# The first strip's output projection of layer one, moved from an even unit into the odd unit behind it, with its sum kept on chip for layer two

## The chip, the cores and the metric

The kernel runs on one core of a Trainium2 chip. Five engines work side by side, each on its own stream of instructions: TensorE (PE in the profile; its weight loads are PEld), VectorE (DVE), ScalarE (ACT), GpSimd (POOL) and SyncE (SP), which here only issues DMAs. The metric is the device time of one execution in microseconds; of several runs the median is given.

## The reference, cut to what matters

The input x has 8 images of 384 channels and 64 x 64 points, in float32. Two layers follow each other, each with a residual and a group normalisation (groups of 12 channels over all points of an image) in front:

- Layer one: `x = x + L0(gn(x))`. L0 normalises every point over its channels, makes q, k and v with one matrix, and does attention in 8 x 8 windows with 8 heads. Half of the heads use plain windows; the other half use windows shifted by 4 rows and 4 columns, with wrap-around and a mask. The two halves are joined and go through a 384 x 384 output projection, `out @ proj_w + proj_b`.
- Layer two: `x = x + L1(gn(x))`. L1 is a 1 x 1 convolution, a filter in the frequency domain of 8 x 8 patches, a 3 x 3 convolution per channel, a gate `gelu(x1) * x2`, and a 1 x 1 convolution back.

What matters here: the group normalisation of layer two needs the mean and the variance of a whole image of layer one's result. Layer two of an image can begin only when the last of its points has gone through layer one's output projection, residual included.

## The kernel before, in words

An image is cut into 8 strips of 8 rows. A strip is a tile of 128 partitions x 3 x 512 floats (768 KB). A strip of layer one has two branches, the plain windows (br 0) and the shifted ones (br 1). One branch of one strip is a *unit*; 16 units make an image, and unit 2s + br of an image belongs to strip s and branch br. Below, units of image b are counted from `first = 16 b`, and the units 16, 17 and 18 of an image are the units 0, 1 and 2 of the next one: there layer one of the next image runs while layer one of this image is completed. Layer two of image b runs two units and more behind its layer one, beside layer one of image b + 1.

The order of the work is a written plan. `at(place, piece, *args)` puts a piece (a small function) at a place, a number in units. All pieces are sorted by place and called in that order. Matmuls stay in exactly that order, since `matmul` marks each with `keep_in_program_order`; the instructions of the other engines are ordered by a scheduler of the framework, which follows the plan and its own estimates. [...]

The pieces of a unit of layer one: `qk_tile` (pq, three tiles of three matmuls, which ACT moves out with their bias), `v_tile` (pvv), `scores` (pS), `weights` and `exponent` (the softmax, on DVE and ACT, tile e), `turn` (transpose, pT), `apply` (pA), `normalise` (DVE: rc and o) and `put` (transpose, po, copied into oT). Ahead of it, once in a strip, `group_normal` reads a loaded strip x_norm and makes y (line 328), `ln_square` makes sq (ACT and POOL), `ln_sums`, `ln_scale` and `shifted_half` finish the normalised strip. The pieces of layer two: `normal_x1` (ACT: xn from x_mix, line 574), `mix` (pt), `transform` (pf), `back` (pz, moved by ACT into z), `conv` (DVE: zz, line 673, eight instructions per third of a strip), `gate` (g) and `finish` (pw, added by DVE onto x_finish, line 712, and stored).

The pieces around the change:

- `load(b, s, what)` takes a new tile out of the pool with tag x (5 buffers) and issues a DMA of 768 KB on SyncE's queue (line 309). The kinds are stats, norm and add (from the input x) and mix and finish (from x1d, the result of layer one, kept in DRAM). Most transfers wait for one ACT instruction of each unit, the second move of the unit's first pq (`zs["gate"]`), so that they start in dense matmul work.
- `project(b, s, m)` does a third of the output projection: three matmuls into pr, and one DVE instruction that adds bias and residual in x_add (line 546).
- `keep(b, s)` takes the statistics of the strip with three DVE instructions (st, line 237); `store(b, s)` writes the strip to x1d (line 556).
- `second_mean(b)` closes the statistics: DVE makes mv_b (line 244), TensorE multiplies it with a group matrix (pm_b, one small matmul), DVE makes gt_b. `second_std(b)` multiplies again (pv_b), ACT takes the root (sd_b), DVE makes gs_b and sh.

Why strip 0 is late: the shifted windows of the last strip wrap around into strip 0, so oT of strip 0 is complete only in unit 16. The strips 0 and 7 of an image are both projected there:

```python
places = [first + 2 * NS + f + (0.0 if s else 0.24) for f in (0.36, 0.44, 0.52)]
```

The pools set further conditions. PSUM has four banks for all tiles made by `psum` (pq, pvv, pr, pt, pf, pz, pm_b, pv_b and the first two thirds of pw), used in turn, and two double banks made by `psum2` (pS, pT, pA, po and the last third of pw), also in turn. A tile's first matmul waits until the tile that had its bank before has been read.

TensorE's stream also holds no-ops (`nc.tensor.nop`). The planner at the end of the function counts TensorE's instructions and spreads empty ones over the tiles of pq and pr, so that the runs of many small matmuls (ln, pf, pz, pA, pS) begin at a chosen place within blocks of 256 instructions.

Of the kernel before, what the change touches and what calls it, by code (L numbers as in the profile page):

```python
# [18 lines left out]
NS = SW // WS  # L19
# [19 lines left out]
def block_kernel(ctx: ExitStack, tc: tile.TileContext, out, x, consts, fsel, wqk, wv, bqk, bv,  # L39
                 wp, bp, lng, lnb, rpb1, rpb2, w_in, w_dw, w_out, filt):  # L40
    nc = tc.nc
    B = x.shape[0]
# [32 lines left out]
    def strip(tag, bufs, name):  # L75
        return sb.tile([P, KC, ST], F32, tag=tag, bufs=bufs, name=name)
# [7 lines left out]
    def rows_of(img, s):  # L84

        return img[:, s * WS:(s + 1) * WS, :].rearrange("(p k) h w -> p k (h w)", k=KC)
# [190 lines left out]
    def at(place, piece, *args):  # L277
        plan.append((place, len(plan), piece, args))

    xs, ys, y2s, qks, vs, os_, ots, x1s, zs = ({} for _ in range(9))  # L280
# [12 lines left out]
    def in_dense_work(i):  # L293


        if zs.get("gate"):
            behind(i, zs["gate"], mybir.DependencyClass.Sync, "transfer in dense work")
# [4 lines left out]
    def load(b, s, what):  # L302

        if b == 0 and (what == "stats" or what == "norm" and s < 3):
            xs[b, s, what] = first_x[s]
            return
        t = xs[b, s, what] = strip("x", 5, f"x_{what}_{b}_{s}")
        src = x1d[b][s] if what in ("mix", "finish") else rows_of(x[b], s)
        in_dense_work(nc.sync.dma_start(out=t, in_=src))
# [411 lines left out]
    for b in range(B):  # L721
        first = 2 * NS * b

        for s in range(NS):
            u = first - 14.84 + s if b else -10 + 0.1 * s
            at(u, load, b, s, "stats")
            at(u + (0.5 if b else 0.05), input_stats, b, s)
        if b == 0:
            at(-3.02, pack_qk)
            at(-2.9, qk_weights, 0)  # L730
            at(-0.95, v_weights)
            at(-0.94, qk_weights, 1)
            at(-0.9, position_bias, 0)
            at(-0.5, position_bias, 1)
            at(0.2, out_bias)
            at(0.2, filter_weights)
        at(first - 5.8 if b else -8, input_mean, b)
        at(first - 5.4 if b else -7.9, input_std, b)
        for s in range(NS):
            u = first + 2 * s  # L740

            v = u - 4
            at(v - 0.84, load, b, s, "norm")
            at(v + 0.15, group_normal, b, s)
            at(v + 0.45, ln_square, b, s)
            if b:
                at(v + 0.985, small_tiles, v + 1)
            at(v + 0.99, ln_sums, b, s)
            at(v + 1.35, ln_scale, b, s)

            if s:
                at(v + 1.50, shifted_half, b, s - 1, 1)
            else:
                at(u - 1.15, shifted_half, b, NS - 1, 1)
            at(u - 1.2 if s < NS - 1 else v + 1.55, shifted_half, b, s, 0)
            for br in range(2):
                w = u + br
                for t in range(3):
                    at(w - 1 + (0.14, 0.34, 0.55)[t], qk_tile, b, s, br, t)
                for g in range(2):  # L760
                    at(w - 1 + ((0.78, 0.86), (0.67, 0.88))[br][g], v_tile, b, s, br, g)
                at(w + 0.05, scores, b, s, br)
                at(w + 0.12, weights, b, s, br)
                at(w + 0.30, exponent, b, s, br)
                at(w + 0.64, turn, b, s, br)
                at(w + 1.00, apply, b, s, br)
                at(w + 1.07, normalise, b, s, br)
                at(w + 1.23, put, b, s, br)

            if 0 < s < NS - 1:  # L770
                places = [u + 3 + f for f in (0.27, 0.45, 0.70)]
            else:
                places = [first + 2 * NS + f + (0.0 if s else 0.24) for f in (0.36, 0.44, 0.52)]
            at(int(places[0]) - 0.84, load, b, s, "add")
            for m in range(KC):
                at(places[m], project, b, s, m)
            at(places[2] + 0.1, keep, b, s)
            at(int(places[2]) + 1.15, store, b, s)
        first += 2 * NS
        at(first + 1.25, second_mean, b)  # L780
        at(first + 1.90, second_std, b)
        if b == B - 1:
            at(first + 2, tap_matrices)
        for s in range(NS):
            u = first + 2 + 2 * s
            at(u - 0.84, load, b, s, "mix")
            at(u + 0.02, normal_x1, b, s)
            for i in range(4):
                at(u + (0.28, 0.45, 0.60, 0.78)[i], mix, b, s, i)
            for j in range(2):  # L790
                at(u + (0.995, 1.02)[j], transform, b, s, j)
            if b < B - 1:
                at(u + 1.985, small_tiles, u + 2)
            at(u + 1.99, back, b, s)

            for n, m in enumerate((0, 2, 1)):
                for tap in range(1, 6):
                    at(u + (2.62, 3.15, 3.5)[n] + 0.06 * tap, conv, b, s, m, tap)
                for tap in range(6, 9):
                    at(u + 4.2 + 0.25 * (n * 3 + tap - 6) / 9, conv, b, s, m, tap)  # L800
            if b == B - 1:
                at(u + 2.3, conv_taps, b, s)
            at(u + 5.16, load, b, s, "finish")
            at(u + 4.5, gate, b, s)
            at(u + 6.10, finish, b, s)
# [130 lines left out]
```

## Time and profile before

| what | value |
|---|---|
| median of 3 runs | 3713.88 us (3712.17 to 3715.45) |
| the profiled execution, whole | 3717.37 us |
| its span in the profile | 3715.4 us |
| granted TensorE clock | 0.995 |
| DMA | 377.34 MB, mean 102 GB/s |
| DVE: one zz (line 673) | 751 ns, 1490 of them |
| DVE: one x_add with pr (line 546) | 747 ns, 192 of them |
| DVE: one st of x_add (line 237) | 689 ns median |
| DVE: mv_b (line 244) | 805 ns |
| DVE: one y (line 328) at the boundary | 541 ns median |
| store of x1d, loads of x_mix | 64 each, 768 KB each |

The profile is one execution, taken by the hardware. Busy times are per engine; a line number is that of the kernel shown here. Because of the helper `matmul`, all matmuls have line 62 and all transposes line 72, so groups are told apart by their tiles: `pr<-oT,wp_sb` is pr written from oT and wp_sb. A float32 matmul stands as two records, so a tile of three matmuls is x6. The ends of matmuls are modelled, so TensorE's time is best read from the start of one tile to the start of the next. Consecutive instructions on DVE overlap a little at their ends too, and their cost is the step from start to start. A wait is put down to whoever released it last. The chain of waits goes back from an end to what released each step, and "issue" in it is time in which nothing visible was waited for.

### The profile page before, as it was taken

What the parts mean: (1) busy time and instruction counts of PE and PEld (TensorE: products, weight loads), DVE (VectorE), ACT (ScalarE), POOL (GpSimd) and SP (SyncE); (2) the same over time, 40 slices, a digit from 0 to 9 for tenths busy, and PEclk for the clock granted to TensorE, in tenths of its full rate; (3) what the DMA queues carried; (4) which work ended last, traced back from release to release, by engine and by line L of the source; (5) the groups of instructions that cost most, each with busy time, mean ns of one, the idle gap of its engine ahead of it and who ended that gap; (6) DMA issues with size and microseconds to landing.
All of it is one profiled execution on the core that took longest, in us unless ns stands there. A gap on an engine that the chain in (4) does not pass through costs nothing.

```text
span 3715.4 us, 92922 instructions
## 1 busy us (share of the span) xinstructions
PE 3609.1 (97%) x38528; PEld 2340.4 (63%) x38528; DVE 2844.0 (77%) x4601; ACT 2383.0 (64%) x3946; POOL 435.1 (12%) x776
## 2 busy tenths in 40 slices
PE   4999999999999999999999999999999999999898
PEld 2666666666666666666666666666666666666554
DVE  4555568777887788787887778877788777777898
ACT  1766676666676576675776667676676766676442
POOL 5111111011111011101111011111011111110000
PEclk9999999999999999999999999999999999999999
DMA  4222222233232233222332332323232322222422
GB/s 122 80 89 75 92 100 102 87 111 109 101 123 84 89 134 109 104 94 104 107 130 84 109 106 101 132 82 105 88 131 102 107 89 84 100 81 81 154 103 77
DMA packets 144507, 377.34 MB, mean 102 GB/s; under 512 B 12308, under 2 KB 12900, under 8 KB 144100
## 3 DMA queue, kind: packets, MB, share of 16 engines
q1 hardware_dynamic: 139952, 370.60, 28.4%
q8 instruction: 319, 5.23, 0.6%
q0 software_dynamic: 2048, 0.15, 0.1%
q10 hardware_dynamic: 2100, 0.63, 0.1%
q14 instruction: 88, 0.72, 0.1%
HBM read 270.54 MB, written 100.79 MB: 100 GB/s over the span
## 4 chain that ended last, share of the span: by engine, by line
PE 86%; DVE 6%; DMA 4%; ACT 2%; issue 1%; POOL 0%; SPq 0%; DVEq 0%; ACTq 0%; POOLq 0%
PE pq L62 24%; PE pr L62 13%; PE pvv L62 12%; PE pt L62 12%; PE pw L62 6%; DVE zz L673 3%; PE pS L62 3%; PE pA L62 3%; PE pT L72 3%; PE po L72 3%; PE pz L62 3%; PE pf L62 2%; PE ln L62 2%; DMA x_norm<-in_x_dram 1%; DMA rpb_raw<-in_rpb_dram 1%
## 5 line engine op out<-in xcount | busy, mean ns | idle before, releaser
L673 DVE SCALAR_TENSOR_TENSOR zz<-z,dw_sb,zz 128x512 f32<-128x512 f32 x1490 | 1081.8, 751 | 23.7 <-ACT z L632 11.2
L62 PE MATMUL pq<-y,wqk_sb 128*128 128x512 f32 x2160 | 990.2, 596 | 0.0
L62 PEld LDWEIGHTS pq<-y,wqk_sb 128*128 128x128 f32 x2160 | 402.7, 190 | 437.1 <-issue 403.9
L62 PE MATMUL pt<-wi_sb,xn 128*128 128x384 f32 x1536 | 534.6, 486 | 0.0
L62 PE MATMUL pr<-oT,wp_sb 128*128 128x512 f32 x1152 | 523.1, 592 | 0.4 <-DVE oT L537 0.4
L62 PE MATMUL pvv<-wv_sb,y 128*128 128x192 f32 x2880 | 495.8, 326 | 0.0
L62 PEld LDWEIGHTS pvv<-wv_sb,y 128*128 128x128 f32 x2880 | 471.7, 190 | 36.2 <-issue 22.0
L394 ACT ACTIVATE qab<-pq,bq_sb,cst 96x512 f32<-96x512 f32 (+1 forms) x256 | 197.8, 772 | 401.9 <-PE pq L62 385.0
L62 PEld LDWEIGHTS pt<-wi_sb,xn 128*128 128x128 f32 x1536 | 286.1, 190 | 200.9 <-issue 44.0
L394 ACT ACTIVATE kcd<-pq,vec 32x512 f32<-32x512 f32 x512 | 348.4, 680 | 9.0
L62 PEld LDWEIGHTS pr<-oT,wp_sb 128*128 128x128 f32 x1152 | 211.1, 190 | 223.8 <-issue 212.3
L376 POOL COPY y<-y 128x384 f32<-128x384 f32 x112 | 100.0, 893 | 1529.4 <-PE pvv L62 1035.9
L335 POOL TENSOR_TENSOR sq<-sq 128x512 f32<-128x512 f32 x128 | 164.3, 1283 | 638.2 <-ACT sq L333 633.3
L584 ACT COPY t<-pt 128x384 f32<-128x384 f32 x256 | 124.1, 485 | 177.7 <-PE pt L62 174.5
L667 ACT ACTIVATE zz<-z,dw_sb 128x512 f32<-128x512 f32 x183 | 134.0, 733 | 159.0 <-PE pw L62 144.5
L349 DVE TENSOR_TENSOR lr<-m 128x128 f32<-128x128 f32 x64 | 19.7, 308 | 278.3 <-ACT m L347 278.3
L394 ACT ACTIVATE qcd<-pq,bq_sb,cst 96x512 f32<-96x512 f32 (+1 forms) x256 | 197.1, 770 | 44.4 <-PE pq L62 40.9
L428 ACT COPY v<-pvv 128x384 f32<-128x384 f32 x256 | 120.7, 477 | 160.2 <-PE pvv L62 159.2
L546 DVE SCALAR_TENSOR_TENSOR x_add<-pr,vec,x_add 128x512 f32<-128x512 f32 x192 | 143.4, 747 | 94.3 <-PE pr L62 92.6
L62 PE MATMUL pw<-zz,wo_sb 128*128 128x512 f32 (+1 forms) x512 | 182.4, 499 | 0.0
L394 ACT ACTIVATE kab<-pq,vec 96x512 f32<-96x512 f32 (+1 forms) x256 | 174.2, 680 | 9.0 <-PE pq L62 7.4
L72 PEld LDWEIGHTS pT<-cst,e 128*128 128x128 f32 x1024 | 119.1, 141 | 67.2 <-issue 39.8
(140 smaller groups left out, 5297.2 us busy)
## 6 DMA issues: line engine op xcount, KB each, us to landing
x_add<-in_x_dram SPq DMA_DIRECT2D x64, 768.0 KB
x1d<-x_add SPq DMA_DIRECT2D x64, 768.0 KB
x_mix<-x1d SPq DMA_DIRECT2D x64, 768.0 KB
x_finish<-x1d SPq DMA_DIRECT2D x64, 768.0 KB
out_dram<-x_finish SPq DMA_DIRECT2D x64, 768.0 KB
x_norm<-in_x_dram SPq DMA_DIRECT2D x61, 768.0 KB
x_stats<-in_x_dram SPq DMA_DIRECT2D x56, 768.0 KB
rs<-line SPq DMA_DIRECT2D x62, 256.0 KB
```

Source lines behind the costliest of these rows:

```text
L62: tc.keep_in_program_order(nc.tensor.matmul(*args, **kw))
L72: tc.keep_in_program_order(nc.tensor.transpose(*args, **kw))
L335: nc.gpsimd.tensor_tensor(sq[:, 0, :], sq[:, 0, :], sq[:, k, :], ALU.add)
L349: nc.vector.tensor_tensor(rc, m[:, 0:P], m[:, 0:P], ALU.mult)
L376: nc.gpsimd.tensor_copy(dst[:, :, :, :, 0:4], src[:, :, :, :, 4:8])
L394: return nc.scalar.activation(dst[to:to + n], pq[of:of + n], AF.Identity, bias=bias[of:of + n], scale=scale)
L428: nc.scalar.copy(v[:, 2 * g:2 * g + 2, :, 0:HD], pvv[:, 0:384].rearrange("p (g h d) -> p g h d", g=2, h=4))
L546: nc.vector.scalar_tensor_tensor(t[:, m, :], pr, bp_sb[:, m:m + 1], t[:, m, :], ALU.add, ALU.add)
L584: nc.scalar.copy(t1, pt[:, 0:C])
L667: nc.scalar.activation(zz.rearrange("p (r c) -> p r c", c=SW), z[:, 1:9, 1:SW + 1], AF.Copy, scale=dw_sb[:, m, 4:5])
L673: i = nc.vector.scalar_tensor_tensor(acc.rearrange("p (r c) -> p r c", c=SW), z[:, dy:dy + 8, dx:dx + SW], dw_sb[:, m, TAPS[tap]:TAPS[tap] ...
```

## The change

For all images but the last, the projection of strip 0 moves from unit 16 to unit 17: its three parts from the places 16.60, 16.68 and 16.76 to 17.20, 17.32 and 17.45. What hangs on these places moves along: the load of x_add for strip 0 from 15.16 to 16.16, its statistics (`keep`) from 16.86 to 17.55, its store from 17.15 to 18.15. `second_mean` moves from 17.25 to 17.57, behind the new `keep`; `second_std` stays at 17.90. The load of x_mix for strip 0 is left out: `normal_x1` reads the tile x_add of strip 0, which is still on chip, and the store to x1d stays, since `finish` reads it much later. The last image keeps the old places.

```diff
         if b == 0 and (what == "stats" or what == "norm" and s < 3):
             xs[b, s, what] = first_x[s]
+            return
+        if what == "mix" and s == 0 and b < B - 1:
+            xs[b, s, what] = xs[b, s, "add"]
             return
         t = xs[b, s, what] = strip("x", 5, f"x_{what}_{b}_{s}")
         src = x1d[b][s] if what in ("mix", "finish") else rows_of(x[b], s)
...
             if 0 < s < NS - 1:
                 places = [u + 3 + f for f in (0.27, 0.45, 0.70)]
+            elif s == 0 and b < B - 1:
+                places = [first + 2 * NS + 1 + f for f in (0.2, 0.32, 0.45)]
             else:
                 places = [first + 2 * NS + f + (0.0 if s else 0.24) for f in (0.36, 0.44, 0.52)]
             at(int(places[0]) - 0.84, load, b, s, "add")
...
             at(int(places[2]) + 1.15, store, b, s)
         first += 2 * NS
-        at(first + 1.25, second_mean, b)
+        at(first + (1.25 if b == B - 1 else 1.57), second_mean, b)
         at(first + 1.90, second_std, b)
```

In the built program the scheduler also moves work of other pieces at these boundaries. On DVE, y of the next image's strip 3 goes from behind the odd unit's zz to a place between x_add's second and third part, and the statistics of x_stats move from unit 18 into unit 17. On ACT, sq of that strip moves ahead of the evictions of the third pq, and the table load for the exponent follows DVE's e.

## The prediction

> **What bounds the kernel now.** I read the page's busy times first, then TensorE's waits, then the stages at an image boundary, then the chain of waits there. The page:
>
> ```profile
> PE 3609.1 (97%) x38528; PEld 2340.4 (63%) x38528; DVE 2844.0 (77%) x4601; ACT 2383.0 (64%) x3946; POOL 435.1 (12%) x776
> ```
>
> TensorE is busy for 97% of 3715.4 us, and the change adds and removes no matmul. It can only gain or lose through TensorE's idle time. Who ended that idle time (waits of PE over the whole run: total us, times, longest):
>
> ```profile
> PE pT L72 <- ACT e L469: 9.9, 8, 1.5
> PE pz L62 <- ACT v L428: 6.9, 13, 1.0
> PE pw L62 <- DVE o L504: 6.1, 6, 1.3
> PE pS L62 <- issue: 2.7, 5, 0.9
> ```
>
> The rest of that list belongs to the start and to the last image. These four stand at the image boundaries. I take the boundary behind the fourth image as the pattern (the others repeat it) and split it into the even unit that holds the projection now, the odd unit that gets it, and the two units behind. Windows: us, then busy time of PE, PEld, DVE, ACT, POOL, clock, DMA share, GB/s:
>
> ```profile
> 1703.80:1748.80 45.00, 45.00 (x348) 26.34 (x342) 30.08 (x50) 21.30 (x42) 3.48 (x10) 1.00 0.09 36
> 1748.80:1767.70 18.90, 18.00 (x290) 13.37 (x283) 17.06 (x28) 14.13 (x21) 2.62 (x4) 1.00 0.73 259
> 1767.70:1798.60 30.90, 29.90 (x318) 19.52 (x314) 25.59 (x46) 25.07 (x42) 3.88 (x7) 1.00 0.16 57
> 1798.60:1818.00 19.40, 17.82 (x288) 12.69 (x284) 18.63 (x27) 13.27 (x19) 2.47 (x3) 1.00 0.50 177
> ```
>
> The even unit has no idle TensorE and DVE and ACT with 15 and 24 us to spare; the odd unit is short on TensorE, nearly full on DVE (17.06 of 18.90) and full of DMA (0.73). TensorE idles 0.90, 1.00 and 1.58 us in the last three. The first two in TensorE's timeline:
>
> ```profile
> 1764.97 2.02 PE L62 MATMUL pz<-cst,t 64*64 64x64 f32 x93 [0.90 <-ACT v L428]
> ...
> 1770.77 0.66 PE L62 MATMUL pw<-g,wo_sb 64*64 64x256 f32 x8 [1.00 <-DVE o L504]
> ```
>
> The 0.90: ACT starts the odd unit's exponent only at 1757.51, then works through seven evictions of pq and one of pT, and frees pvv's bank too late. The 1.00 has a longer story, which the chain of waits through this stage tells (start, us, what):
>
> ```profile
> 1753.50 0.78 ACT qab L394
> ...
> 1754.29 3.28 DMA x1d<-x_add
> ...
> 1757.59 0.32 SPq L309
> ...
> 1757.95 9.96 DMA x_norm<-in_x_dram
> ...
> 1768.01 1.46 DVE y L328 x3
> ...
> 1769.67 0.97 DVE o L504
> ...
> 1770.77 3.44 PE pw L62 x16
> ```
>
> The store of strip 0 must land before SyncE issues x_mix of strip 0; x_norm is issued behind it and is the fifth of six transfers of 768 KB; DVE stands in y until x_norm is there; o waits behind y; pw waits for o.
>
> [...] o stands behind y on DVE though its pA was done at 1767.90, and no matmul passed the waiting pw. So a pm_b that waits holds all of TensorE. [...] the zz at 1757.40 takes 0.99 us instead of the row's 751 ns, while POOL copies y from 1756.41 to 1757.84. [...]
>
> **The change part by part.** T is the start of the odd unit's first pq, 1749.83. All sums are for one boundary; seven boundaries have the change, six of them with both layers running.
>
> *Matmuls of pr.* Three tiles of three matmuls, each tile 2.57 us (pr 1683.23, next tile 1685.81), go from the even to the odd unit: minus 7.7 and plus 7.7, sum 0. In the built program the total of PE no-ops is the same (3902); the planner spreads the odd unit's 30 over six tiles instead of three. One more PE wait instruction per image shifts where the small matmuls fall in the instruction stream by up to six; the even unit's run goes from place 180 to 145 of 256, where the like runs of the other strips stand (140 to 147). [...] I take 0, bounds minus 2 and plus 3 us for the run.
>
> *The even unit without pr.* DVE loses three x_add, three st and mv_b, all in idle stretches there (3.7 and 3.9 us idle before them). Its last tiles of pt and pvv keep their distances to their evictions, so no new wait: 0.
>
> *The load of x_mix for strip 0.* Its data were never late: xn ran 1768.00 to 1770.89 and its first pt started at 1777.50, so 6.6 us cover it. Removing it is worth nothing by itself. Its place in SyncE's queue is worth something: the store of strip 0 moves a unit back, x_mix goes, and x_norm is third behind one store and x_finish. Where three loads go in that order in later odd units, the third has landed between T+13.0 and T+14.1 (in the trace's completion marks; here x_norm came at T+18.1). The built order has DVE's y and ACT's sq of that strip one unit earlier too, before the boundary.
>
> *pz, 0.90.* With 7.7 us more TensorE work in the odd unit, ACT evicts pq as it comes (second pq ends T+11.4, third T+16.6). By my count its first pvv eviction ends at T+22.3, while pz needs it at T+23.9. Gone. Over six boundaries the gaps are 0.70, 0.71, 0.90, 0.97, 0.87, 0.98: minus 5.1 us.
>
> *pw, 1.00.* y is now done long before o. From pA's end DVE needs rc 0.25 and o 0.96 plus about 0.25 of hand-over, 1.5 us; TensorE has 1.85 us of pS and pw in between. Other even units with that distance show 0.1. The gaps 1.26, 1.20, 1.00, 0.90, 1.07, 0.71 sum to 6.1; minus 5.5 us.
>
> *pm_b, the new wait.* It stood behind the even unit with mv_b done at 1744.04, 9.3 us early. Now it follows the third pq, with mv_b behind the last x_add. TensorE reaches it at T + 2.68 + 5 x 2.57 + 0.87 = T+16.4. DVE: e ends at T+7.65 as before (same rows ahead of it). Then in the built order x_add, zz, st, zz, zz, x_add, zz, st, zz, y x3, x_add, oT, st, zz, mv_b. Steps from start to start, read from the same mix at 1689 to 1697: 0.66 after x_add or zz, 0.60 after st, 0.79 between dependent zz, 0.45 for y[...]. That brings y to T+13.8 (just after x_norm has landed), the last x_add to T+15.2, its pr being ready at T+14.0, mv_b to T+17.8; with 0.81 us it ends at T+18.6. TensorE waits 2.2 us. Bounds: 1.0 with every step at its shortest[...], 3.5 if x_norm lands at T+14.1[...]. Queued behind pm_b are pT, pvv and pz; they move by the same 2.2, and DVE and ACT catch up meanwhile, so nobody behind waits anew: sd comes at T+25.9, xn some 6 us before its pt. Six boundaries: plus 13.2 us. The first boundary has no layer two beside it (no zz); its mv_b ends near T+17.4: plus 1.0.
>
> *Store a unit later.* It delays x_stats in the unit behind by about 2 us; DVE has 3.7 us idle at 1793.09 to cover it: 0. The pT wait of the fourth unit (1.3) follows from rs, y and e of that unit, which stay as they are: 0.
>
> Sum: 13.2 + 1.0 - 5.1 - 5.5 = **plus 3.6 us**. The profiled span of 3715.4 becomes 3719.0. The profiled execution took 3717.37 us around its span; the median of the runs is 3713.88, 3.5 lower. I add the same 3.6 to the median: 3717.5 us, 0.1%. A measurement of this kernel tells about 0.2% (7.4 us) from no change.
>
> **The rivals.** *A, the trade (0.65):* two waits out, one in, as above; within 0.2% while the pm_b wait is between 0.4 and 2.8 us. *B, x_norm becomes the stall (0.28), slower:* y stands in DVE's queue ahead of the last x_add, so every us that x_norm lands behind T+13.8 adds a us to pm_b, at six boundaries. For it: the margin is half a us at best, and ACT's sq stands ahead of the qcd evictions too. Against: two of the four transfers ahead of it are gone. From T+14.4 on it is over 0.2%; at today's T+18.1 it would be 3.6 + 6 x 4.3, plus 29 us, 3743. Landing at T+15.3 gives 3726. *C, the gain is kept (0.07), faster:* DVE gets mv_b done before TensorE comes, minus 10.6 us, 3703. For it: x_add, st and mv_b alone, each dependent on the one before (0.79 + 0.79 + 0.81), would end 2.4 us after pr at T+14.0, just when TensorE comes. Against: that needs a free DVE at T+14.0, and it has y, oT and a zz to do in between. *D, the change does not reach the waits* (in B's share): pz and pw keep theirs since ACT's burst stays; then plus 14, 3728.
>
> Range: 3708 to 3727; it holds A with its bounds (1.0 and 3.5 of wait give minus 3.6 and plus 11.4) and the nearer half of B. Faster 0.07, same 0.65, slower 0.28.
>
> **What would show it.** Right: PE waits list pm_b <- DVE mv_b with some 14 us in 6 or 7 times, 2 to 2.5 each; the rows pz <- ACT v and pw <- DVE o lose some 5 us each; pT stays near 9.9; even unit near 37.3 us, odd near 28. DVE shows y without an idle before it in the odd unit. Wrong: y waiting for x_norm (B), pm_b without a wait (C), or new "issue" gaps in the small matmuls (the stream's places).

## The result, and the profile after

The changed kernel takes 3722.73 us (median of 12 runs, 3718.51 to 3728.0). The kernel before, run beside it, takes 3712.52 us (12 runs, 3707.72 to 3715.45). The ratio is 1.0028, with a 95% interval of 1.0020 to 1.0036: 10.2 us slower, between 7 and 13. Repeated later (e5) it was 3723.94 against 3713.37, 1.0029 (1.0018 to 1.0040). The prediction was 3717.5 us in a range of 3708 to 3727. The measured time lies in the range, and the trade that was forecast (two waits out, one in) came, but its size was not right: plus 3.6 us was forecast, and the change costs 0.28%, more than the 0.2% that can be told from no change.

The profiled execution took 3723.41 us around a span of 3721.6. Its difference to the profiled span before (3715.4) is only 6.2 us. That is no contradiction: the profiled execution before, 3717.37 us, lay 4.9 us above the median of its own kernel, the one after 0.7. So I compare the terms in the traces, and take sizes from the medians.

TensorE's busy time differs by 0.7 us from before (3609.1), with the same 38528 matmul records:

```profile
PE 3609.8 (97%) x38528; PEld 2342.4 (63%) x38528; DVE 2844.6 (76%) x4601; ACT 2386.4 (64%) x3946; POOL 436.2 (12%) x776
```

Who ended TensorE's idle time, kernel after (total us, times, longest):

```profile
PE pm_b L62 <- DVE mv_b L244: 16.9, 7, 2.6
...
PE pT L72 <- ACT e L472: 9.3, 8, 1.5
...
PE pS L62 <- issue: 3.9, 7, 0.9
...
PE pz L62 <- ACT v L431: 1.8, 7, 0.3
```

The row pw <- DVE o (6.1 us) is gone, pz lost 5.1 us of its 6.9, and pm_b (the matmul that closes the statistics) stands there new with 16.9. The four units at the boundary behind the fourth image, which the prediction used as its pattern (us, then busy time of PE, PEld, DVE, ACT, POOL, clock, DMA share, GB/s):

```profile
1707.50:1744.80 37.30, 37.30 (x331) 22.95 (x326) 24.98 (x43) 20.28 (x38) 1.78 (x8) 1.00 0.18 64
1744.80:1773.10 28.30, 25.66 (x310) 16.57 (x306) 25.28 (x41) 15.85 (x22) 5.48 (x6) 1.00 0.37 122
1773.10:1802.60 29.50, 29.50 (x312) 19.46 (x307) 22.74 (x39) 23.76 (x41) 1.33 (x5) 1.00 0.24 82
1802.60:1822.10 19.50, 17.91 (x292) 12.77 (x286) 18.70 (x27) 13.27 (x19) 2.47 (x3) 1.00 0.50 177
```

The even unit lost its 7.7 us, the odd one grew from 18.90 to 28.30 and now holds the idle time, and the unit behind it shrank from 30.9 to 29.5. DVE is busy 25.28 of 28.30 us in the odd unit. Here is what it does there before pm_b, with T = 1745.80, the start of the first pq (start, us, what), and then the wait on TensorE:

```profile
1759.33 1.46 DVE L331 TENSOR_SCALAR y<-x_norm,gs_a 128x512 f32<-128x512 f32 x3
1760.71 0.74 DVE L549 SCALAR_TENSOR_TENSOR x_add<-pr,vec,x_add 128x512 f32<-128x512 f32 x1
1761.48 0.69 DVE L531 COPY oT<-po 64x512 f32<-64x512 f32 x1
1762.21 0.69 DVE L237 BATCH_NORM_STATS2 st<-x_add 128x6 f32<-128x512 f32 x1
1762.82 1.44 DVE L676 SCALAR_TENSOR_TENSOR zz<-z,dw_sb,zz 128x512 f32<-128x512 f32 x1
1764.18 0.79 DVE L244 BATCH_NORM_AGGREGATE mv_b<-st 128x2 f32<-128x144 f32 x1
```

```profile
1765.03 0.38 PE L62 MATMUL pm_b<-mv_b,cst 128*128 128x1 f32 x2 [2.64 <-DVE mv_b L244]
```

y starts without an idle before it, the last x_add at T+14.9, mv_b ends at T+19.2, and TensorE had nothing to do from T+16.6 on. The sequence is the one forecast; one zz in it takes 1.44 us.

One thing has no counterpart in the waits. The odd unit lasts 28.2 to 28.3 us in four of the six images that have both layers, but 30.00 and 29.91 us in the third and the fifth (the second and fourth of these six), with no more idle time. Windows of 3.4 us through the third image's odd unit show it in the clock column:

```profile
1313.60:1317.00 3.40, 3.05 (x8) 1.02 (x6) 3.34 (x6) 3.06 (x5) 0.29 (x1) 1.00 0.28 110
1317.00:1320.40 3.40, 1.11 (x10) 1.11 (x11) 3.37 (x6) 1.97 (x3) 2.56 (x2) 1.00 0.00 0
1320.40:1323.80 3.40, 3.40 (x13) 3.40 (x12) 3.37 (x8) 1.01 (x1) 0.00 (x0) 0.50 0.02 5
1323.80:1327.20 3.40, 3.40 (x81) 3.38 (x81) 0.77 (x2) 1.44 (x3) 0.00 (x0) 0.99 0.00 0
```

TensorE is idle for 2.3 of the 3.4 us in the second window (the pm_b wait), and for the whole third window the granted clock is 0.50. TensorE is "busy" there and does half the work: the pvv matmuls behind the wait (24 records) take 5.74 us where they take 4.07 us at the fourth image:

```profile
1320.44 5.74 PE L62 MATMUL pvv<-wv_sb,y 128*128 128x192 f32 x24
...
1766.18 4.07 PE L62 MATMUL pvv<-wv_sb,y 128*128 128x192 f32 x24
```

That is 1.7 us more, with no entry in any list of waits.

### The profile page after: what moved, and what is told of

It reads as the page before. It is cut to its first block, busy times and chain, and to the rows that moved or that the text cites. A ratio compares the mean times of both kernels' runs of the same rounds, so it can differ in the third digit from the quotient of the medians.

```text
span 3721.6 us, 92896 instructions
## 1 busy us (share of the span) xinstructions
PE 3609.8 (97%) x38528; PEld 2342.4 (63%) x38528; DVE 2844.6 (76%) x4601; ACT 2386.4 (64%) x3946; POOL 436.2 (12%) x776
## 4 chain that ended last, share of the span: by engine, by line
PE 86%; DVE 8%; DMA 2%; ACT 2%; issue 2%; POOL 0%; SPq 0%; ACTq 0%; DVEq 0%; POOLq 0%
PE pq L62 25%; PE pvv L62 13%; PE pt L62 12%; PE pr L62 12%; PE pw L62 6%; DVE zz L676 4%; PE pS L62 3%; PE pA L62 3%; PE pz L62 3%; PE pT L72 3%; PE po L72 3%; PE pf L62 2%; PE ln L62 2%; DMA rpb_raw<-in_rpb_dram 1%; DMA rs<-line 1%
```

## The experiments

Each row has the kernel before as it ran beside it on the same chip.

| run | median us (runs) | before | ratio (95%) | pm_b wait, sum, us | half clock, windows of 3.41 us, images 2 to 7 |
|---|---|---|---|---|---|
| after | 3722.73 (12) | 3712.52 | 1.0028 (1.0020 to 1.0036) | 16.9 | 2 |
| e5 after again | 3723.94 (7) | 3713.37 | 1.0029 (1.0018 to 1.0040) | 16.9 | 1 |
| e1 wait filled | 3721.45 (21) | 3713.76 | 1.0020 (1.0013 to 1.0026) | 1.6 | 0 |
| e9 a third filled | 3724.75 (7) | 3713.75 | 1.0030 (1.0019 to 1.0042) | 11.7 | 2 |
| e10 wait lengthened | 3749.61 (4) | 3713.75 | 1.0097 (1.0084 to 1.0111) | 32.6 | 10 |
| e4 mean first on DVE | 3711.31 (21) | 3713.76 | 0.9992 (0.9986 to 0.9999) | 7.4 | 0 |
| e8 a load put back | 3713.75 (13) | 3713.37 | 1.0002 (0.9994 to 1.0010) | 8.8 | 0 |
| e2 pm_b later | 3709.14 (21) | 3713.76 | 0.9987 (0.9980 to 0.9993) | 0.2 | 0 |
| e6 e2 with places | 3704.46 (11) | 3713.37 | 0.9976 (0.9967 to 0.9985) | 0 | 0 |
| e7 after with places | 3722.93 (9) | 3713.37 | 1.0027 (1.0017 to 1.0036) | 17.0 | 4 |
| e3 sum kept, no move | 3714.74 (13) | 3713.76 | 0.9999 (0.9991 to 1.0007) | none | 0 |
| e11 e3, o first on DVE | 3706.44 (19) | 3712.86 | 0.9984 (0.9977 to 0.9991) | none | 0 |

The last two columns are from the one profiled execution of each. The halved windows are those between the first 110 us and 3480 us; before and after have others outside that stretch (clock 0.50 from 65 to 78 us in both).

### The clock: e1, e9, e10, e5

Theory: a wait of 2.6 us costs more than 2.6 us, since the clock may be halved behind it, as at 1320.4 us above. Three edits vary the idle time at pm_b and leave its place in the order as it is.

e1 fills the wait with matmuls of constants:

```diff
         pm = psum(f"pm_{name}")
+        for _ in range(fill):
+            matmul(pm, ident, cst[:, 0:ST], start=True, stop=True)
         matmul(pm[:, 0:1], grp, mv[:, 0:1], start=True, stop=True)
...
-        gs1[b] = group_mean(st1s.pop(b), f"b{b}")
+        gs1[b] = group_mean(st1s.pop(b), f"b{b}", 3 if 0 < b < B - 1 else 0)
```

> The kernel after, with three matmuls of constants (128x512 each, overwritten by the mean that follows) in front of pm_b in images two to six, where TensorE waits 2.48 to 2.64 us for mv_b. They take 2.57 us, as long as the wait. Theory 1, the clock: what the prediction missed is the granted clock, halved for 3.41 us after some of the waits, each time worth 1.7 us, in between none and six boundaries of one execution. Then no stretch of half clock is left between the first 100 us and 3480 us, the time falls by 1.7 us for each one taken away, to 3717 to 3720 us (the fastest execution of the kernel after was 3718.5), and its executions agree as closely as those of before (within 8 us, not 9.5). Theory 2, the clock is no matter and the rest is scattered over issue gaps: unchanged, 3722 to 3723 us.

Measured: 3721.45 us, no half clock in the middle of the run, and odd units of 28.2 to 28.8 us in all six images. (The expectations of e1, e9 and e10 name images two to six; the edits cover two to seven, six boundaries.) The trace agrees with the theory; the median does so only weakly. It is 7.7 us above before, where the kernel after was 10.2 and 10.6 above: 2.5 to 2.9 us gained, although the filled units are some 0.3 us longer than unhalved ones of after. But the intervals of the ratios overlap, it missed its 3720, and its runs still spread over 7.4 us.

e9 fills only a third:

```diff
-        gs1[b] = group_mean(st1s.pop(b), f"b{b}", 3 if 0 < b < B - 1 else 0)
+        gs1[b] = group_mean(st1s.pop(b), f"b{b}", 1 if 0 < b < B - 1 else 0)
```

> The kernel after, with one matmul of constants (0.87 us) in front of pm_b in images two to six instead of three: TensorE then idles 1.6 to 1.8 us at pm_b and not 2.6, the end of the unit stays where it is. In the profiled executions so far a free-running window of 3.41 us was followed by half clock when it held 1.79 to 2.38 us of idle, and was not at 1.66 to 1.77 (once 1.79 was, once 1.85 was not). Theory 1: an idle stretch of 1.8 us or less can't reach that in any window, so no half clock is left and the time is that of the kernel with three, 3719 to 3722 us, lost idle or not. Rival: each idle us counts toward the clock, and it lies halfway to the kernel after.

This one missed. The waits fell to 1.63 to 1.82 us, and still two windows of half clock came, behind windows that held 1.70 and 1.69 us of idle; the odd units of those two images took 29.92 and 29.90 us, the others 28.2 to 28.6. The time, 3724.75 us, is no better than after. The third image's window and the one behind it:

```profile
1315.20:1318.60 3.40, 1.70 (x12) 1.30 (x12) 3.37 (x5) 1.86 (x3) 2.37 (x2) 1.00 0.00 0
1318.60:1322.00 3.40, 3.40 (x13) 3.40 (x12) 3.33 (x9) 1.01 (x1) 0.00 (x0) 0.50 0.02 5
```

So the limit is lower than I had set it. I laid the grid of 3.413 us that the clock records give over the profiles of after, e5, e7 and e9: in images two to seven, windows with 1.69, 1.70, 1.79, 2.01, 2.19, 2.19, 2.28 and 2.38 us of recorded idle were followed by half clock, while windows with 1.66 to 1.77, and one with 1.85, were not. The least idle time followed by half clock is 1.69 us, about half of the window, but the idle time that the profile records for a window does not settle it alone up to about 2 us; e10 has an exception at 1.99.

e10 makes mv_b later:

```diff
         strip_stats(st1s[b], s, xs[b, s, "add"])
+        for _ in range(3 if s == 0 and 0 < b < B - 1 else 0):
+            nc.vector.bn_stats(st1s[b][:, KC - 1, :], xs[b, s, "add"][:, KC - 1, :])
```

> The kernel after, with the last st of strip 0 written three more times in images two to six (the same values), so that mv_b comes some 3 us later (the order then also sets three st of x_stats ahead of it): a pm_b wait of about 5.5 us instead of 2.6. Theory 1 (wait plus clock): at each of those five boundaries one or two windows of half clock, 5 to 9 in all instead of 2; 3722.7 + 5 x 2.9 + 4 to 12 = 3741 to 3749 us, and a narrower spread than after. Rival (the wait alone): 3737 us, and the number of halved windows doesn't grow.

The scheduler also set three st of x_stats ahead of mv_b, as the expectation names. This dose separates the theories. Windows through the second image's odd unit:

```profile
873.80:877.20 3.40, 0.00 (x0) 0.00 (x0) 3.40 (x7) 0.86 (x2) 1.25 (x1) 1.00 0.00 0
877.20:880.60 3.40, 2.73 (x12) 2.73 (x13) 3.32 (x8) 0.24 (x1) 0.00 (x0) 0.51 0.02 5
880.60:884.00 3.40, 3.40 (x12) 3.40 (x12) 0.36 (x2) 0.77 (x1) 0.00 (x0) 0.50 0.00 0
884.00:887.40 3.40, 3.40 (x89) 3.38 (x89) 0.00 (x0) 1.73 (x3) 0.00 (x0) 0.99 0.00 0
```

The time grew by 26.9 us to 3749.61, the pm_b wait by only 15.7 (16.9 to 32.6). The wait alone would have given 3738. The six odd units together grew from 172.9 to 200.4 us, by 27.4; what the waits leave is 11.7 us, for 8 more windows of half clock (10 instead of 2), 1.5 us each. That is a little less than 1.7: four of the ten windows also hold 0.53 to 1.62 us of the idle time itself. At the fourth image a window with 1.99 us of idle was not followed by half clock; that came only behind the next one, which was idle throughout:

```profile
1771.53:1774.94 3.41, 1.42 (x4) 0.35 (x2) 3.35 (x6) 3.24 (x4) 1.88 (x2) 1.00 0.00 0
1774.94:1778.35 3.41, 0.00 (x0) 0.00 (x0) 3.41 (x7) 0.36 (x1) 0.65 (x1) 1.00 0.00 0
1778.35:1781.76 3.41, 3.34 (x14) 3.34 (x15) 3.08 (x9) 0.85 (x1) 0.00 (x0) 0.50 0.02 5
```

Behind a window that was halved already a second one came with less idle time: with those 0.53 to 1.62 us at four of the six boundaries, and in e7 with 0.30 us at one.

e5 is the kernel after once more.

> The kernel after, unchanged, beside the kernel before on one chip with more executions. Theory 1 (the clock is halved after a random number of the pm_b waits): its profile shows some stretches of half clock between 100 and 3480 us, not the two at the same places, and the median is 3721 to 3725 us, 8 to 10 above before. If the two stretches come at the same boundaries again, their number is a property of the program and not of the execution.

Its profile had one such window, behind the fourth image, where the first profile had none. Whether a wait is hit is thus a property of the execution, and the runs of after spread over 9.5 us.

### DVE's order: e4 and e8

The prediction said why the wait is there: DVE has y, oT and a zz to do between the last pr (T+14.0) and mv_b. e4 sets y (the first i) and that zz (the second) behind mv_b:

```diff
+            if b and s == 3:
+                behind(i, zs["aggr"], mybir.DependencyClass.NoSync, "mean first")
...
+        if b < B - 2 and s == 6 and m == 1 and tap == 1:
+            behind(i, zs["aggr"], mybir.DependencyClass.NoSync, "mean first")
```

> The kernel after, with DVE's order in the odd unit changed: the three y of strip 3 and the zz of the second channel block stand behind mv_b instead of ahead of it. Theory 1: the sum's own chain (x_add, st, mv_b behind the last pr at T+14.0, with oT and one st of x_stats between) ends near T+17.4, TensorE comes at T+16.6, so the pm_b wait falls from 2.6 to about 0.9 us, too short for the clock to be halved: 3722.7 - 6 x 1.65 - 4 = 3709 us. Rival: the wait is the chain's own length or x_stats' landing, so it stays over 2 us and the time over 3718.

Measured 3711.31 us, 2.4 us below before where after lay 10 above, with waits of at most 1.1 us and no half clock (waits of PE):

```profile
PE pm_b L62 <- DVE mv_b L244: 7.4, 7, 1.1
```

So the order on DVE made most of the wait, 2.5 to 2.6 us at a boundary before; the 1.1 that stay are the sum's own chain with oT and one st of x_stats in it. It missed its 3709 by 2 us, which its interval (3708.6 to 3713.4 us) leaves open.

e8 puts a load of 768 KB, which nothing reads, back where x_mix of strip 0 was issued:

```diff
+        t = strip("x", 5, f"x_{what}_{b}_{s}")
         if what == "mix" and s == 0 and b < B - 1:
             xs[b, s, what] = xs[b, s, "add"]
+            in_dense_work(nc.sync.dma_start(out=t, in_=rows_of(x[b], s)))
             return
```

> The kernel after, with a load of 768 KB put back where x_mix of strip 0 stood, which nothing reads. The planner then believes x_norm later and sets y behind mv_b on DVE. Theory 1: it is DVE's order that sets the pm_b wait, so it falls to about 1 us and the clock stays whole, though more is transferred: 3709 to 3713 us. Rival B of the prediction: x_norm, now about 2 us later, is waited for ahead of the mean or right behind it, and the kernel is slower than after: 3725 to 3740 us.

With more transferred the kernel is faster than after, 3713.75 us: the scheduler then puts y behind mv_b by itself, and the waits sum to 8.8 us. Against e4, which has a similar order and no such load, it is 2 to 3 us slower. How much of that is the transfer and how much the order is not shown.

### The place of pm_b, and the places in the instruction stream: e2, e6, e7

e2 leaves mv_b where it is (`second_aggregate` is that one DVE instruction), and lets TensorE ask for it later:

```diff
-        at(first + (1.25 if b == B - 1 else 1.57), second_mean, b)
-        at(first + 1.90, second_std, b)
+        at(first + (1.25 if b == B - 1 else 1.57), second_aggregate, b)
+        at(first + (1.25 if b == B - 1 else 1.82), second_mean, b)
+        at(first + (1.90 if b == B - 1 else 2.01), second_std, b)
```

> The kernel after, with mv_b at its place on DVE, but its matmul pm_b behind the first pvv tile and pv_b behind pA (3 and 6 us later on TensorE). Theory 1 (wait and clock): the pm_b row (16.9 us) goes but for the last image and image one, the halved stretches with it (two, 3.4 us, in the profiled execution), and pz and pw stay without their waits; 3722.7 - 15.3 - 4 = 3703 us, 9 to 10 us under the kernel before. Rival: the odd unit is short of DVE and ACT, not only of mv_b; then pv_b, pz or pt take over the wait, some 2 us at six boundaries, and it stays above 3712.

Measured 3709.14 us: 4.6 us below before, but 6 us short of the 3703. The pm_b wait is gone, no other wait took it over (pz and pT stay at 1.8 and 9.9 us), and no half clock is left. What is missing is spread over even units of the later images (6, 8, 10 and 12 are 0.3 to 1.0 us longer), such as unit 6 of the eighth image, which runs beside layer two of the seventh (TensorE's timeline):

```profile
3196.53 1.51 PE L62 MATMUL pw<-g,wo_sb 64*64 64x512 f32 x13
3198.38 0.64 PE L62 MATMUL pw<-g,wo_sb 64*64 64x256 f32 x2 [0.35 <-issue]
```

That unit took 30.57 instead of 29.58 us, in a stretch where TensorE waits for nothing visible. e2 has three more instructions per image in TensorE's stream than the planner counts, and by the count of the built program its runs of small matmuls drift by three places per image, in these units from 18 to 36 of 256. e6 counts them (and fills up the runs of the second image too):

```diff
-            n = (RUN_AT[args[0] % 2] - count - round(WAITS[0] * args[0] + WAITS[1])) % 256
-            if n < 100:
+            more = 0.1875 * max(args[0] - 17, 0)
+            n = (RUN_AT[args[0] % 2] - count - round(WAITS[0] * args[0] + WAITS[1] + more)) % 256
+            if n < (120 if args[0] == 19 else 100):
```

> The kernel with pm_b behind the first pvv tile and pv_b behind pA, with the planner's no-ops set anew: its count of wait instructions grows by 3 more per image, and the runs of the second image are filled up too, so that pS stands at places 16 to 21 and 139 to 143 of 256 in all images, where it drifted by 3 per image to 37 and 160. Theory: [...] then they go and it takes 3703 to 3706 us. Rival: those units are longer for another reason; then 3709 as before.

Measured 3704.46 us, as expected; that unit has 29.58 us again. This version beats both kernels, the one before by 8.9 us and the one after by some 19.

e7 does the same to the kernel after (its drift is one place per image, so 0.0625 stands in place of 0.1875).

> The kernel after, with the no-ops set so that the runs of small matmuls stand at the same places in all images (its own drift is one place per image, 19 to 24), and those of the second image, which the change moved from 250 and 50 to 29 and 86 of 256, stand at 143 and 20. Theory: the new issue gaps of image two (0.91 and 0.94 us) come from these places: 1.3 to 2 us faster than the kernel after, 3720.5 to 3721.5. Rival: the places of the other images count as well (3 us or more), or not at all.

In the trace the gap of the second image is gone: its unit 4 takes 25.71 us as before the change, where after had 26.97. The median fell by 1.0 us against e5, which these runs can't tell from nothing, and this profile happened to have four windows of half clock. Worth 1.3 us in the trace, not resolved in the time.

### What the parts are worth alone: e3 and e11

e3 is the kernel before with only the kept sum and without the load of x_mix:

```diff
+        if what == "mix" and s == 0 and b < B - 1:
+            xs[b, s, what] = xs[b, s, "add"]
+            return
```

> The kernel before, with nothing of the change but the sum kept on chip: strip 0's project and its store stay in the even unit, x_mix of strip 0 is not loaded. SyncE's queue then no longer stands behind the landing of that store, and x_norm is third of four loads. Theory 1: y stops waiting in the odd unit, the pw wait (6.1 us over six boundaries, 7.7 us with what hangs on it) goes, pz keeps its 5.1, no pm_b wait comes: 3705 to 3707 us. Rival: o was late for DVE's own queue and not for x_norm; then 3712 to 3713, as before.

No gain: 3714.74 us, a ratio of 0.9999. x_norm did land earlier, at T+16.0 instead of T+18.1, and y no longer waits. But DVE's timeline there (T = 1747.56) shows what took its place ahead of o:

```profile
1764.76 0.53 DVE L331 TENSOR_SCALAR y<-x_norm,gs_a 128x512 f32<-128x512 f32 x1
...
1765.51 1.88 DVE L237 BATCH_NORM_STATS2 st<-x_stats 128x6 f32<-128x512 f32 x3 [0.16 <-DMA x_stats<-in_x_dram]
1767.31 0.24 DVE L506 RECIPROCAL rc<-pA 128x16 f32<-128x16 f32 x1
1767.58 0.96 DVE L507 TENSOR_TENSOR o<-pA,rc 128x768 f32<-128x768 f32 x1
```

The scheduler moved the three st of x_stats, whose load landed at T+17.9, ahead of o. DVE is idle before them for no more than 0.27 us at any of the five boundaries with this order, but they take 1.88 us. The row pw <- DVE o stays at 6.0 us. e11 forbids that order; `after` is the o of unit 17, for the three st of strip 0:

```diff
+            if after:
+                behind(i, after, mybir.DependencyClass.NoSync, "o first")
...
-            at(u + (0.5 if b else 0.05), input_stats, b, s)
+            at(u + ((0.5 if s else 0.95) if b else 0.05), input_stats, b, s)
```

> The kernel before with the sum kept on chip (as in the run that had no gain), and the three st of x_stats at the image boundary set behind o on DVE. In that run y no longer waited for x_norm, but the three st, whose x_stats landed at T+17.9, took its place ahead of o. Theory 1: it is the wait for a load ahead of o in DVE's queue that pw pays, whichever load; then the pw row (6.0 us, with the time that hangs on it some 7) goes and pz keeps its 6.9: 3707 to 3709 us. Rival: o is late for pA or for DVE's amount of work; then 3714 as in that run.

The row is gone, pz keeps its wait, and the kernel takes 3706.44 us, 6.4 us less than before (waits of PE):

```profile
PE pT L72 <- ACT e L474: 9.9, 8, 1.5
PE pz L62 <- ACT v L433: 6.2, 13, 0.8
PE pw L62 <- DVE g L693: 5.8, 1, 5.8
```

(The remaining pw row is one wait in the last image, which every version has.) The pw wait therefore comes from what stands ahead of o in DVE's queue: before, y, held up by its load (idle 0.45 to 1.0 us, then 1.46 us of work); in e3 three st, which cost o their own 1.88 us far more than a wait for a load. The expectation's theory, that it is the load, fits only the first. Most of what the change gained at pw can be had without moving a matmul.

## Why the prediction was right or wrong, point by point

| term | predicted us | profile after, us |
|---|---|---|
| pm_b wait, six boundaries | +13.2 | +15.3 |
| pm_b wait, first boundary | +1.0 | +1.6 |
| pz | -5.1 | -5.1 |
| pw, with its unit | -5.5 | -7.7 |
| pT | 0 | -0.6 |
| places of the small matmuls | 0 | +1.3 |
| half clock | not in the sum | +3.4 (two windows) |
| sum | +3.6 | +8.2 |

- *Even unit, pr tiles, pz and pT, and the case against B and D:* right. The even unit takes 37.30 us. x_norm landed at T+13.4 and y followed at T+13.5, so the stall of B did not come; both old waits went, so D did not either. That B stayed out was luck in part: over five boundaries x_norm landed at T+12.9 to T+13.4, between 0.1 and 0.5 us ahead of y, and at the third image y waited 0.17 us for it. Against C the prediction argued that DVE is not free at T+14.0; e4 shows that freeing it takes 11 to 13 us off, of the 20 between after and C's 3703.
- *The term that failed: "TensorE waits 2.2 us ... plus 13.2 us".* It prices a wait at its own length. The waits were 2.48 to 2.64 us, so the length was short by 0.35 on average, because the zz ahead of mv_b took 1.44 to 1.55 us, with POOL adding sq beside it, where the mean of all zz is 0.75. They lie within the bound of 3.5. That POOL's adds made the zz longer is not shown, only that they ran at the same time. POOL at the fourth image:

```profile
1762.45 2.93 POOL L338 TENSOR_TENSOR sq<-sq 128x512 f32<-128x512 f32 x2 [5.43 <-ACT sq L336]
```

But the larger miss is that some of the new waits were followed by 3.41 us at a clock of 0.50. The profiles of after, e5 and e7 had two, one and four such windows, 1.7 us each. The prediction's windows of before all show the clock at 1.00, and it has no term for the clock; the old waits at the boundaries, at most 1.5 us, were not followed by half clock.
- *pw:* the size was short by 2.2 us, the unit behind gained more than its recorded idle time (7.7 against 6.1). The explanation was half right. In the changed kernel y comes ahead of everything in time, but e3 shows that an earlier x_norm alone frees nothing, because other work takes its place in DVE's queue.
- *Places of the small matmuls:* put at 0 with bounds of -2 and +3; in the profile before, the "issue" waits of pS and pA sum to 2.7 + 0.8 us. It is plus 1.3 us in the second image, whose runs moved from 250 and 50 to 29 and 86. e6 took back 4.3 us of e2, 1.3 of it in that image; the rest goes with a drift of 18 places by the end. So the place of small matmuls within 256 cost these 4.3 us; why it does, no run shows.

The terms add up to 8.2 us. The spans of the two traces differ by 6.2: the other units, and the start, are some 2 us shorter in the trace of after, in pieces of up to 0.5 us, as they also differ between after and e5, which are the same kernel. The measured difference of the medians is 10.2, with 7.4 to 13.4 as its interval. The 2 us on either side I can't assign: the number of halved windows changes from execution to execution (two in the profile of after, one in e5), and one profile holds one draw.

Of the chances, "within 0.2%" (0.65) did not come true. "Slower" (0.28) did, but through the trade of A and not through B, to which that chance was given. That the time lies in the range is luck in part: pw gained 2.2 us more than forecast, which paid for most of the 2.7 us by which the pm_b waits came out longer, and the upper half of the range had been set without the clock in mind.

## What to carry to other kernels

When TensorE gets a new wait, don't price it at its length alone. Here waits of 1.63 to 1.82 us were followed by 3.41 us of half clock at two of six boundaries, whose units took 29.9 us instead of 28.2 to 28.6 (e9), and the longer waits of e10 cost 11.7 us beyond their length. No list of waits shows that, only the clock column does. A small matmul that needs a statistic belongs behind work that doesn't (e2 and e6, 4.6 and 8.9 us below before), and DVE's order ahead of it should be read instruction by instruction, since the scheduler moves other work there when the loads around it change (e3, e8). A removed stall is only gone when nothing stands ready to take its place in the same queue, as the three st of e3 did with their 1.88 us.

## What the runs showed of the hardware that I had not expected

- The granted clock falls to 0.50 for whole windows of 3.413 us: in the profiles of before and after, all its changes lie on one grid of that step (in after, 1320.43 and 2211.31 us are 261 windows apart). It came behind waits of about 1.7 us (e9) and of 2.48 to 2.64 us (after). In images two to seven a window at full clock was followed by half clock only if it held at least 1.69 us of idle time; up to 1.99 us that did not happen each time, from 2.01 us on it did.
- A DVE zz beside POOL's adds of sq took 1.44 to 1.55 us, where the mean of all zz is 0.75, at all six boundaries of after.
- In e2, even units of the last two images with the drift grew by up to 1.0 us when their small matmuls stood some 15 to 18 of 256 places later, most of it not recorded as idle time.
